# A 5x5 grouped convolution on sixteen tiles of TensorE: one product of each round cut in two

## The chip, the cores and the metric

The kernel runs on one core of a Trainium2 chip. The metric is the time of one execution on the device, in microseconds (us); the time given is the median of several executions. A profile is one more execution, recorded instruction by instruction. PE is TensorE (its matmuls; PEld are its weight loads), DVE is VectorE, ACT is ScalarE, POOL is GpSimd, and SP is the engine that issues most of the transfers.

## What is computed

Two layers work on an image of 4 batches, 512 channels and 64 x 64 pixels. The change lies in the first, a linear attention with two sets of heads: one set comes from a 1x1 projection of the image, the other from that projection after a 5x5 depthwise convolution and a small grouped 1x1 convolution:

```python
q, k, v = h @ wq.T, h @ wk.T, h @ wv.T
qkv = concatenate([q, k, v])
dw = conv(qkv, dw_kernel, groups=3 * 512)        # 5x5, one kernel per channel
pw = conv(dw, pw_kernel, groups=3 * 64)          # 1x1, within a head of 8 channels
f = concatenate([qkv, pw]).reshape(B, heads, 24, N)
query, key, value = relu(f[:, :, :8]), relu(f[:, :, 8:16]), f[:, :, 16:]
scores = einsum('bhdn,bhen->bhde', value_with_ones, key)
out = einsum('bhde,bhen->bhdn', scores, query)
out = out[:, :, :-1] / (out[:, :, -1:] + EPS)
y = x + batchnorm(proj_kernel applied to out)
```

The second layer takes edge filters of y, mixes them with 1x1 products, and normalises over the channels.

## The kernel before

The channels of the first layer are worked on in 16 groups (4 batches by 4 groups of 16 heads). For each group the kernel projects keys and values (`project`, L262, and `values`, L285), then queries, eight strips of 512 pixels each. `project` also writes each strip into an image `inp` with borders (L283), for keys and for queries; the convolution reads that image. For values no convolution is made: a correlation with the convolved keys takes its place (`correlate`, L447, with `weigh`, L469).

`convolve` (L394) computes one half of the image of 32 channel sets at once. It runs four times in each group (keys and queries, two halves), so 64 times in all. It takes four banks of PSUM from a pool of four (`quad_tiles`, tag "quad"), the same four buffers that `correlate` and `spread_out` use. The depthwise 5x5 and the 1x1 kernel are folded into one set of weights (`mat`, built on POOL at L247). Ten rounds follow, for five horizontal shifts `dx` in the order 0, -2, -1, 1, 2 and two vertical blocks `b`. A round is sixteen products of 32 x 32 weights: head set i (0 to 3) reads partitions 32i to 32i+31, pixel set j writes partitions 32j to 32j+31 of bank i. So each of the sixteen products of a round works on its own 32 x 32 tile of the array, and the sixteen can run at the same time; the next round works on the same sixteen tiles. A product covers eight rows of 64 columns (512), or of 62 or 63 where the shift cuts off the edge (496, 504). All numbers are 32 bit, and the trace shows each product as two pairs of a weight load and a matmul, a first and a second pass; hence 20480 records for 10240 products. Below, tile n is the tile of the n-th product of a round, counted from 0.

After the ten rounds ScalarE reads the four banks (L415 for keys, in eight parts, with sums; L421 for queries, in four).

The order of PE's work is written out by hand: `keys_and_values` (L563) and `queries` (L593) list the steps, and after each step `advance` lets the stages that trail behind (projection of the heads L661, edge branches L738, fusing L848) issue a share of their own products, by fixed costs. The convolution's cost in these lists is a constant (T_CONV), so the order depends on no measured time. The last part of the kernel, from about 4.35 ms, has no convolution in it.

Of the kernel before, what the change touches and what calls it, by code (L numbers as in the profile page):

```python
# [50 lines left out]
KV_ORDER = (1, 0, 2, 3, 4, 5, 6, 7)  # L51
Q_ORDER = (6, 7, 5, 4, 3, 2, 1, 0)
DXS = (0, -2, -1, 1, 2)
VROW = 4 * 66


# [27 lines left out]
def _span(d, n):  # L84

    return max(0, -d), n - max(0, d)
# [3 lines left out]
def conv_seq_kernel(  # L90
    ctx: ExitStack, tc, x, wqkv, dpk, wtab, proj, projc, pwk, bn0, consts, vec, watt1, batt1, watt2, wbr, wfuse, out
):
    nc = tc.nc
# [15 lines left out]
    def work_tile(name, n=512):  # L109
        return work.tile([P, 512], F32, tag="w", name=name)[:, :n]  # L110
# [4 lines left out]
    def quad_tiles(name):  # L115
        return [psum.tile([P, 512], F32, tag="quad", name=name) for _ in range(4)]

    def squares(ap):

        return ap.rearrange("p (b x n) -> p n x b", b=4, n=4)  # L120

    def rows(ap, width=W):
        return ap.rearrange("p (r c) -> p r c", c=width)
# [21 lines left out]
    inps = {}  # L145
# [15 lines left out]
    def near_border(v):  # L161

        zeros = vals.tile([P, 8 * VROW], F32, name="zeros", tag="vals")
        nc.gpsimd.memset(zeros, 0.0)
        cols = v.rearrange("a b x r d -> (a b) x (r d)")
        for at in (0, W + 2):
            nc.sync.dma_start(out=cols[:, at : at + 2, :], in_=zeros[0 : 2 * NB, 0 : 2 * VROW])
        for b, r in ((0, 0), (NB - 1, 2)):
# [54 lines left out]
    first = ExitStack()  # L223
    x_first = first.enter_context(tc.tile_pool(name="x_first", bufs=12, side="right"))

    class Group:
# [167 lines left out]
        def convolve(self, t, half):  # L394
            banks = quad_tiles("cv")
            last = len(DXS) * 2 - 1
            for n, (dx, b) in enumerate((dx, b) for dx in DXS for b in range(2)):
                c0, c1 = _span(dx, W)
                for j in range(4):
                    for i in range(4):  # L400
                        q = slice(32 * i, 32 * i + 32)
                        nc.tensor.matmul(  # L402
                            rows(banks[i])[32 * j : 32 * j + 32, :, c0:c1],
                            lhsT=self.mat[t][q, j, (dx + 2) * 8 + 4 * b : (dx + 2) * 8 + 4 * b + 4, :],
                            rhs=inps[t][q, j, 8 * half + b : 8 * half + b + 8, c0 + dx : c1 + dx],
                            start=(n == 0), stop=(n == last),
                        )
            outs = []
            for i in range(4):
                o = work_tile("co")  # L410
                if t == KEY:
                    if half == 0 and i == 0:
                        self.ksum = mini.tile([P, 4, 4], F32, name="ksum")
                    for a in range(2):
                        nc.scalar.activation(  # L415
                            o.rearrange("p (n a x b) -> p a n x b", n=4, a=2, b=4)[:, a],
                            squares(banks[i][:, 256 * a : 256 * a + 256]), AF.Relu,
                            accum_out=self.ksum[:, 2 * half + a, i : i + 1],
                        )
                else:  # L420
                    nc.scalar.activation(o, banks[i], AF.Relu)  # L421
                outs.append(o)
            self.conv[t] = outs
# [10 lines left out]
        def load_near(self, count):  # L434

            for _ in range(count):
                half, jp, b = at = next(self.nears, (None,) * 3)
                if half is not None:
                    self.near[at] = vals.tile([P, 8 * VROW], F32, name="near", tag="vals")
                    for part in range(4):  # L440
                        v = self.near_dram[jp, 8 * half + b + 4 * (part // 2), 32 * (part % 2)]
                        nc.sync.dma_start(
                            out=self.near[at][32 * part : 32 * part + 32, :],
                            in_=bass.AP(v.tensor, v.offset, [[4 * VROW, 8], [(W + 4) * VROW, 4], [1, 8 * VROW]]),
                        )
# [514 lines left out]
    for n, cur in enumerate(groups):  # L960
# [5 lines left out]
        if n and n % NG == 0:  # L966
            last = groups[n - 1]
# [8 lines left out]
    last = groups[-1]  # L976
# [142 lines left out]
```

## Time and profile before

| | |
|---|---|
| median of three executions | 5017.47 us (5010.55 to 5027.52) |
| the profiled execution, its own time | 5033.35 us |
| its span, first to last instruction | 5031.6 us |
| mean clock that TensorE was granted | 0.971 |
| PE busy, matmuls | 4694.3 us (93%), 46140 records |
| DVE, ACT, POOL busy | 2083.3, 1581.8, 397.3 us |
| products of the convolution (L402) | 20480 records, 728.3 us busy, 36.0 us idle before them |
| weight loads of the convolution (L402) | 20480 records, 419.8 us busy, 313.1 us idle before them |
| 16 DMA engines, mean rate | 172 GB/s |

The page sums up busy time by engine, then gives the costliest groups of instructions: a row names the line, engine and operation, what is written and read, the shape, and the number; then busy time, the mean duration of one, the idle time of the engine ahead of such instructions, and what ended most of it. Matmuls overlap, so busy time is less than number times duration. "issue" as a cause of idle time means that nothing the profile shows was waited for. Other views used below are the answer for one source line, the timeline of a stretch (start, length, engine, line, operation, number, and in brackets the idle time before), and the trace's single records, with the start and length of each weight load, matmul and DMA packet.

### The profile page before, as it was taken

The numbers are of one execution on the slowest core, as the hardware profiler recorded it, in microseconds if no ns is written. First come the engines' busy times: TensorE is split into PE (matmuls) and PEld (weight loads), VectorE is DVE, ScalarE is ACT, GpSimd is POOL, SyncE is SP. The second block draws the span as 40 slices with busy tenths as digits, with TensorE's granted clock in tenths as the row PEclk, the third lists the DMA queues.
The fourth block names the chain that finished last, engine by engine and source line by source line (L and its number), as shares of the span: only waits on it lengthen the run. The fifth ranks groups of instructions, "written<-read, shape, count | busy, mean of one in ns | idle before, by whom it ended". The sixth has DMA issues, their size and how long they took to land. (4 is left out here: it accounts for less than half of the span.)

```text
span 5031.6 us, 106279 instructions
## 1 busy us (share of the span) xinstructions
PE 4694.3 (93%) x46140; PEld 2689.2 (53%) x46140; DVE 2083.3 (41%) x2761; ACT 1581.8 (31%) x2712; POOL 397.3 (8%) x298
## 2 busy tenths in 40 slices
PE   9999999999999999799899999989999899899887
PEld 5655654455666554354465656445446565444333
DVE  1222222115565533311355553441125555447955
ACT  2112111003454423200245442430014445214765
POOL 0000000000000012100000000220000000000445
PEclk9999999999999999899999999999999999899998
DMA  6434467775666566677565566647665555575435
GB/s 198 138 119 134 134 192 194 162 163 161 193 190 189 180 187 189 192 177 167 152 189 189 186 192 183 207 153 217 149 173 176 171 173 170 162 166 144 165 125 163
DMA packets 627940, 864.04 MB, mean 172 GB/s; under 512 B 324073, under 2 KB 381449, under 8 KB 609041
## 3 DMA queue, kind: packets, MB, share of 16 engines
q1 hardware_dynamic: 548880, 756.51, 52.4%
q10 hardware_dynamic: 78592, 100.74, 6.3%
q8 instruction: 362, 5.93, 0.5%
q14 instruction: 106, 0.86, 0.1%
HBM read 575.93 MB, written 213.98 MB: 157 GB/s over the span
## 5 line engine op out<-in xcount | busy, mean ns | idle before, releaser
L268 PE MATMUL proj<-xt,w_sb 128*128 128x512 f32 x2048 | 955.9, 610 | 56.7 <-DMA xt<-in_x 34.6
L661 PE MATMUL yps<-hd,fold_sb 128*128 128x512 f32 x2048 | 907.8, 599 | 18.5 <-DMA hd<-heads 16.2
L402 PE MATMUL cv<-inp,mat 32*32 32x512 f32 x20480 | 728.3, 593 | 36.0 <-issue 28.2
L268 PEld LDWEIGHTS proj<-xt,w_sb 128*128 128x128 f32 x2048 | 382.7, 194 | 528.0 <-issue 451.6
L661 PEld LDWEIGHTS yps<-hd,fold_sb 128*128 128x128 f32 x2048 | 386.1, 191 | 511.0 <-issue 458.8
L402 PEld LDWEIGHTS cv<-inp,mat 32*32 32x32 f32 x20480 | 419.8, 103 | 313.1 <-issue 151.9
L848 PE MATMUL zps<-ef,wf_sb 128*128 128x512 f32 (+1 forms) x1056 | 473.4, 601 | 36.4 <-DMA ef<-ef 19.4
L290 PEld LDWEIGHTS val<-w_sb,xt 128*128 128x128 f32 x4096 | 470.6, 192 | 33.2 <-issue 25.9
L290 PE MATMUL val<-w_sb,xt 128*128 128x128 f32 x4096 | 485.2, 277 | 0.1
L738 PE MATMUL br<-maps,wbr_sb 128*128 128x256 f32 (+1 forms) x1792 | 474.2, 418 | 3.7 <-DVE s_sb L335 2.9
L274 ACT COPY strip<-proj 128x512 f32<-128x512 f32 x256 | 149.3, 583 | 932.5 <-PE proj L268 912.0
L666 DVE SCALAR_TENSOR_TENSOR yt<-yps,shift,xr 128x512 f32<-128x512 f32 x128 | 96.0, 750 | 836.5 <-PE yps L661 780.0
L738 PEld LDWEIGHTS br<-maps,wbr_sb 128*128 128x128 f32 x1792 | 340.9, 193 | 146.9 <-issue 102.0
L457 PE MATMUL corr<-near,ckt 128*32 128x160 f32 x8192 | 333.7, 315 | 40.3 <-DMA near<-near 32.9
L848 PEld LDWEIGHTS zps<-ef,wf_sb 128*128 128x128 f32 x1056 | 205.3, 198 | 285.5 <-issue 235.9
L247 POOL TENSOR_TENSOR mat<-dp_sb 128x1280 f32<-128x1280 f32 x32 | 76.7, 2398 | 3484.8 <-PE cv L402 2882.9
L457 PEld LDWEIGHTS corr<-near,ckt 128*32 128x32 f32 x8192 | 257.2, 111 | 136.1 <-issue 78.6
L714 DVE TENSOR_TENSOR maps<-dv 128x1054 f32<-128x1054 f32 (+1 forms) x112 | 158.0, 1411 | 376.3 <-PE br L738 376.2
L318 ACT ACTIVATE kt<-tr 128x512 f32<-128x512 f32 x128 | 75.9, 593 | 529.8 <-PE tr L316 401.2
L366 DVE RECIPROCAL rec<-rec 128x512 f32<-128x512 f32 x64 | 214.4, 3351 | 1.7
L746 ACT ACTIVATE ef_o<-br,shift,scale 128x256 f32<-128x256 f32 (+1 forms) x224 | 131.4, 590 | 228.1 <-PE br L738 210.4
L415 ACT ACTIVATE co<-cv 128x256 f32<-128x256 f32 x256 | 94.0, 398 | 331.1 <-PE cv L402 310.6
(127 smaller groups left out, 4049.2 us busy)
## 6 DMA issues: line engine op xcount, KB each, us to landing
xt<-in_x SPq DMA_DIRECT2D x316, 512.0 KB
near<-near SPq DMA_DIRECT2D x512, 264.0 KB
inp<-strip ACTq DMA_DIRECT2D x1024, 64.0 KB
win<-y SPq DMA_DIRECT2D x96, 396.0 KB
near<-vt SPq DMA_DIRECT2D x512, 66.0 KB
y<-yt SPq DMA_DIRECT2D x128, 264.0 KB
heads<-q SPq DMA_DIRECT2D x128, 256.0 KB
cheads<-cq SPq DMA_DIRECT2D x128, 256.0 KB
```

What stands on the lines that cost most here:

```text
L268: nc.tensor.matmul(ps, lhsT=self.w[t][:, c, :], rhs=xs[self.b, j][c], start=(c == 0), stop=(c == NCH - 1))
L274: nc.scalar.copy(s, ps)
L290: nc.tensor.matmul(ps[:, ts(c, P)], lhsT=xs[self.b, j][n][:, ts(c, P)], rhs=self.w[VALUE][:, n, :], start=(n == 0), stop=(n == NCH - 1),)
L366: nc.vector.reciprocal(rec, rec)
L402: nc.tensor.matmul(rows(banks[i])[32 * j : 32 * j + 32, :, c0:c1], lhsT=self.mat[t][q, j, (dx + 2) * 8 + 4 * b : (dx + 2) * 8 + 4 * b + 4, :],
L457: nc.tensor.matmul(self.banks[jj][32 * i : 32 * i + 32, 160 * b : 160 * b + 160], lhsT=self.held["c", i][:, at : at + 32], rhs=v[:, 4 * n ...
L661: nc.tensor.matmul(ps, lhsT=fold_sb[g // NG][:, g % NG, ts(c, P)], rhs=hd[g], start=(g == 0), stop=(g == 2 * NG - 1),)
L666: nc.vector.scalar_tensor_tensor(yt[:, :, 1 : W + 1], rows(ps), shift0[:, c : c + 1], rows(xr), ALU.add, ALU.add)
L714: nc.vector.tensor_sub(flat[:, half : 3 * half - 2], dvs[:, 2 : 2 * half], dvs[:, 0 : 2 * half - 2])
L738: nc.tensor.matmul(rows(ps), lhsT=wbr_sb[:, k, c, :], rhs=rows(maps[:, slot[k], c % 2, :], WB)[:, :, 0:W], start=(c == 0), stop=(c == NCH ...
L746: nc.scalar.activation(o[:, n, :], parts[n], AF.Gelu, bias=shift1[:, k : k + 1], scale=scale1[:, k : k + 1], accum_out=pool_sb[:, k, u : u ...
L848: nc.tensor.matmul(ps, lhsT=wf_sb[:, k, ts(c, P)], rhs=ef[k], start=(k == 0), stop=(k == 3))
```

## The change

The first product of each round (i = j = 0) covers all its columns but the last twelve of each of the eight rows. The fifteen others follow unchanged. Then a second product with the same weights covers the twelve columns left over. The start mark stays with the first part in the first round (the second part never carries one), and in the last round the end mark of that tile moves to the second part. Nothing else is edited: other engines' instructions keep their order, and ScalarE's first read of the convolution's banks now waits for the second part, which has become the last product.

```diff
+TAIL = 12
...
         def convolve(self, t, half):
             banks = quad_tiles("cv")
             last = len(DXS) * 2 - 1
+
+            def product(n, dx, b, j, i, c0, c1, first=True, end=True):
+                q = slice(32 * i, 32 * i + 32)
+                nc.tensor.matmul(
+                    rows(banks[i])[32 * j : 32 * j + 32, :, c0:c1],
+                    lhsT=self.mat[t][q, j, (dx + 2) * 8 + 4 * b : (dx + 2) * 8 + 4 * b + 4, :],
+                    rhs=inps[t][q, j, 8 * half + b : 8 * half + b + 8, c0 + dx : c1 + dx],
+                    start=(n == 0 and first), stop=(n == last and end),
+                )
+
             for n, (dx, b) in enumerate((dx, b) for dx in DXS for b in range(2)):
                 c0, c1 = _span(dx, W)
+
                 for j in range(4):
                     for i in range(4):
-                        q = slice(32 * i, 32 * i + 32)
-                        nc.tensor.matmul(
...
-                            start=(n == 0), stop=(n == last),
-                        )
+                        lead = i == j == 0
+                        product(n, dx, b, j, i, c0, c1 - TAIL if lead else c1, end=not lead)
+                product(n, dx, b, 0, 0, c1 - TAIL, c1, first=False)
```

## The prediction

> **What bounds the kernel now.** I read the page first. PE is busy for 93% of the span, DVE for 41%. The convolution's products (L402) are the third costliest group: 728.3 us busy and 36.0 us idle before them. Queue q8, which brings instructions, matters later: 362 packets of 5.93 MB are 16 KB each, 256 instructions of 64 bytes.
>
> ```profile
> span 5031.6 us, 106279 instructions
> ...
> PE 4694.3 (93%) x46140; PEld 2689.2 (53%) x46140; DVE 2083.3 (41%) x2761; ACT 1581.8 (31%) x2712; POOL 397.3 (8%) x298
> ...
> q8 instruction: 362, 5.93, 0.5%
> ...
> L402 PE MATMUL cv<-inp,mat 32*32 32x512 f32 x20480 | 728.3, 593 | 36.0 <-issue 28.2
> ```
>
> Next the answer for L402 alone: its weight loads (PEld) sat idle mostly for "issue", waits that no semaphore explains.
>
> ```profile
>   issue: 180.0, 370
>   DVE weighed L475: 19.9, 30
> ```
>
> Then the timeline of weight loads in one undisturbed convolution: 32 loads in 0.23 us, stops of 0.2 to 0.3 us, and ten rounds done 10.6 us after the start.
>
> ```profile
> 191.67 0.23 PEld L402 LDWEIGHTS cv<-inp,mat 32*32 32x32 f32 x32 [0.17 <-issue]
> 192.13 0.10 PEld L402 LDWEIGHTS cv<-inp,mat 32*32 32x32 f32 x1 [0.22 <-issue]
> 192.56 0.55 PEld L402 LDWEIGHTS cv<-inp,mat 32*32 32x32 f32 x32 [0.32 <-issue]
> 193.42 8.02 PEld L402 LDWEIGHTS cv<-inp,mat 32*32 32x32 f32 x255 [0.31 <-issue]
> ```
>
> Last a disturbed one, which begins at 305.20 and takes 14.9 us: twice PE stops for over 2 us.
>
> ```profile
> 313.71 0.24 PEld L402 LDWEIGHTS cv<-inp,mat 32*32 32x32 f32 x32 [2.17 <-issue]
> ...
> 319.63 0.14 PEld L402 LDWEIGHTS cv<-inp,mat 32*32 32x32 f32 x4 [2.42 <-issue]
> ```
>
> The trace's single records of the 191.68 convolution give the rest. Each product is two pairs of weight load and matmul. A pass streams 0.83 ns a column plus 3 (430 ns for 512 columns, 423 for 504, 416 for 496), and 22 more for the first pass of a product whose tile was already free. When nothing waits, the next product starts 16.6 ns later. But where a product finds its tile of the array busy, the next product starts only 193 ns after that one does: in round 1 the first tile starts at 883 (453 + 430), and the second, free at 890, at 1076. One to three such stops fall in each round, so the last pass starts 10,070 ns after the first (1007 a round), where a tile's own two passes need 832 to 860. Some twenty convolutions show 10,070 to within 2 ns.
>
> [...] second passes of round 0 start at 453 to 553, after first passes of later products. [...] in the 305.20 convolution a packet starts at 311.39, PE stops 0.05 later and resumes at 313.71, 1.45 after the packet landed.
>
> **The change, part by part.** *Removed:* 12 of some 63 columns (8 rows, 96 of 504) from tile 0's leading product. Its two passes become 416, 400 or 408 columns for shifts of 0, 2 and 1: 350, 337, 343 ns. *Added:* one product of 96 columns a round, behind the fifteen; 640 products, 2560 PE instructions on 92,280 (2.8%; 6.25% within a convolution). No DMA, no SP or POOL step moves. ScalarE's first read of a convolution now waits for the tail, the last product, and its later reads have no waits on PE: the four last products it waited for started within 50 ns of each other, so nothing (at most 64 x 50 ns, 3 us, if a read waits for the tail alone).
>
> *A round after.* Tile 0: first pass 22 + 350, second 350; then the tail, queued long before, starts at 722. It is the one product that finds its tile busy. The next round's first product comes 193 later, at 915. The tail itself needs 2 x 83 = 167, up to 211 if each pass pays the 22 (bounds; 33-column passes of L327 follow each other on one tile every 33 ns, 27.5 + 5, so I take 167). So the stop lies over the tail. The second tile is free at 17 + 450 + 430 = 897 and wanted at 932: 35 ns to spare, so no further stop. Rounds: 915, 888, 901 for 512, 496, 504 columns. Start of the last round: 2 x 915 + 2 x 888 + 4 x 901 + 888 = 8098; its sixteenth product starts 249 later and ends after 438 + 416: 9201. Before: 10,070 + 416 = 10,486. **Gain 1.285 us** a convolution. If the tail took 211, the next product would wait too, one more stop per round but at 933 and not at 1007: about 1.0.
>
> *How many get it.* In 17 of the 64, tile 3 starts 0.7 to 4.9 us after tile 0, because its bank waits for VectorE (mostly L475). There the late tile sets the end and tile 0 is ahead: nothing gained. 47 x 1.285 = **60 us**.
>
> *What takes it back: instructions.* A 256-instruction block lasts four rounds, 4.03 us; with 68 a round and 894 ns it lasts 3.37. For the 138 blocks that are used up within a convolution (the block before mostly in it too) I took from the records the time from the previous block's change to 1.4 us after the landing (stopped PEs resumed 1.3 to 1.65 after it). Quartiles: 3.3, 4.0, 5.2 us. 67 of 138 are over 4.03, by 0.62 us in the mean over all; 102 are over 3.37, by 1.02. I hold these fetch times independent of PE's pace. The 47 clean convolutions: 117 blocks x 0.62 = 73 us late before, of which 42 show (they take 515 us against 47 x 10.07 = 473): 0.57 of it, the rest lay under the stops. After: 125 blocks x 1.01 = 126 us, of which 0.57 (72) to all (126) shows. With fewer stops to lie under I take 0.7: 88, a loss of 88 - 42 = **46 us**. The 17 staggered ones run 6.25% more instructions through the same fetch: 17 x 0.16 blocks x 0.7 = **2 us**.
>
> *Sum.* 60 - 46 - 2 = 12 to 13 us off. Against its own execution: 5033.35 us (span 5031.6 and 1.75 around it) becomes 5020.5. That execution stands 0.3% above the median of 5017.47; the same taken from the median gives **5004 us**. PE is the bound on both sides of the convolutions. Waits on PE for x (34.6 us) and near (32.9) could swallow a few us; I take none.
>
> **Rivals.** *Fetch doesn't hold it back* (blocks come sooner when asked sooner, or runs without the profiler fetch faster): up to the whole 60 us, 4957; with a quarter lost, 4972, which I take. For it: some twenty convolutions have no stop for instructions at all. Against: half of the blocks are late already. *Slower: fetch is the bound.* If all lateness shows, 126 - 42 = 84 is lost against 60 gained: 24 and 2 make 5043. It decides once more than 0.8 of the lateness shows, or blocks are over 0.2 us later than above. For it: the 6.25% more instructions come in full, and 102 of 138 blocks would be late. Against: a stop frees all tiles, and part of it stays covered. *The change doesn't do what it says*: another product takes over the 193 ns stop, at the 35 ns margin, every round; then the rounds stay near 1007, and only the fetch of more instructions remains: 5017 to 5022.
>
> **Chances.** Fetch-limited gain 0.50 (4989 to 5014, own range); nearly the full gain 0.27; slower by fetch 0.15; stop taken over 0.08. A measurement of this kernel can tell about 0.3% (15 us) from no change. Faster by more: 0.27 and 0.21 of the first, 0.48. Within: 0.28 of the first and the 0.08, 0.36. Slower: 0.15 and 0.01 of the first, 0.16. The range, 4960 to 5030, leaves out the far ends of the second and third.
>
> **What would show it.** In undisturbed convolutions the last pass starts at about 8870 instead of 10,070; 17 staggered ones keep their length; the "issue" idle of L402's loads loses its 0.2 to 0.3 us pieces and gains in pieces over 1 us; q8 has 10 more packets. I am wrong if rounds don't fall to about 900, if the stops over 1 us neither grow nor multiply, or if they swallow more than 60 us.

## The result, and the profile after

The kernel became slower: 5057.62 us median of four runs (5042.51 to 5065.52), beside 5018.39 us (5010.55 to 5027.52, four runs) for the kernel before. The ratio is 1.0077, with a 95% interval of 1.0058 to 1.0095. The prediction, 5004 us and more likely faster than not, was wrong in sign, and 5057.62 lies above its range.

The page of the changed kernel (the product is at L402 again, by chance; lines ahead of `convolve` stand two higher, later ones nine):

```profile
span 5040.7 us, 108783 instructions
...
PE 4708.8 (93%) x47420; PEld 2667.3 (53%) x47420; DVE 2086.8 (41%) x2761; ACT 1581.3 (31%) x2712; POOL 400.7 (8%) x298
...
q8 instruction: 372, 6.09, 0.5%
...
L402 PE MATMUL cv<-inp,mat 32*32 32x512 f32 (+2 forms) x21760 | 758.2, 573 | 46.1 <-issue 38.3
```

The 1280 added weight loads and 1280 added matmuls and the ten added packets on q8 are there: 256 PE instructions for each added packet of 16,384 bytes, by estimate 64 bytes an instruction. VectorE, ScalarE and GpSimd are busy as long as before. The products of L402 take 30 us more busy time (728.3 to 758.2) and 10 us more idle time (36.0 to 46.1): the loss lies in the convolutions. The two profiled spans differ by 9.1 us only, because the execution profiled before was slower than any timed run of its kernel and the one profiled after the fastest of its own; the medians say 39 us.

The answer for L402 alone says what the loads waited for (us, times):

```profile
  issue: 326.3, 790
  DVE weighed L484: 19.2, 31
```

"issue" goes from 370 pieces of 180.0 us to 790 of 326.3. VectorE is as before. Part of that growth is the view's: this answer leaves out gaps of up to 0.15 us. The page's row for the loads has every gap, and there the idle time rose by 57 us, from 313.1 to 370.1:

```profile
L402 PEld LDWEIGHTS cv<-inp,mat 32*32 32x32 f32 x21760 | 404.9, 103 | 370.1 <-issue 288.0
```

The timeline of weight loads of an undisturbed convolution, one without a stop for instructions or for a late bank, shows where the pieces lie:

```profile
371.24 0.48 PEld L402 LDWEIGHTS cv<-inp,mat 32*32 32x32 f32 x33 [0.17 <-issue]
371.96 0.72 PEld L402 LDWEIGHTS cv<-inp,mat 32*32 32x32 f32 x34 [0.24 <-issue]
372.93 1.31 PEld L402 LDWEIGHTS cv<-inp,mat 32*32 32x32 f32 x37 [0.24 <-issue]
374.44 0.73 PEld L402 LDWEIGHTS cv<-inp,mat 32*32 32x32 f32 x34 [0.20 <-issue]
375.49 0.74 PEld L402 LDWEIGHTS cv<-inp,mat 32*32 32x32 f32 x34 [0.31 <-issue]
376.55 0.74 PEld L402 LDWEIGHTS cv<-inp,mat 32*32 32x32 f32 x34 [0.32 <-issue]
```

Before, this view showed up to three stops at the opening and then 255 loads in one piece. Now every round ends in a stop: 34 loads (17 products) in 0.74 us, 0.32 us of nothing, and again. The period is 1.06 us, where I had predicted 0.89 to 0.92.

The stop itself is neither new nor longer. Before, the loads' waiting was spread over gaps too short for the view. The single records show it: a product that finds its tile idle has a first pass 22 ns longer, and such products begin together behind each stop. In the undisturbed convolutions at 191.68 (before) and 371.24 (after), in ns from the start:

```
                                     before                  after
groups of such products begin at     4243 5303 6364 7424     4253 5313 6374 7436
matmuls from one to the next           34   34   34            34   34   34
groups in the whole convolution        10                      10
matmuls from the last group on         16                      32
```

In both kernels 34 matmuls, 17 products, pass in a period of 1061 ns (at 504 columns). Sixteen products take 16/17 of that, an estimate of 998 ns a round; the prediction's 1007 is the time to the last start divided by ten. Seventeen products take the whole period. Both convolutions need ten periods, and before the last is only half filled, so the last start moves by little.

I call the length of a convolution the time from the start of its first matmul to the start of its last. Twenty of 64 take 10,070 ns before (sum of all 64: 724.8 us); after, nine take 10,217 to 10,230 (sum: 764.8 us). The sum grew by 40.0 us, as much as the medians lost. The single records of the convolution at 371.24, in ns from its start, beside what the prediction's steps say:

```
                              measured   predicted
tile 0, first pass                   0           0
tile 0, second pass                373         372
tail, first pass                   723         722
tail, second pass                  908         805
next round's first product         990         915
next round's second product       1083         932
```

Up to the start of the tail the prediction is within 1 ns. The tail's second pass then starts not 83 ns after its first, when the columns are through, but 185 ns after it.

### The profile page after: what moved, and what is told of

It reads as the page before. It is cut to its first block, busy times and chain, and to the rows that moved or that the text cites. A ratio compares the mean times of both kernels' runs of the same rounds, so it can differ in the third digit from the quotient of the medians.

```text
span 5040.7 us, 108783 instructions
## 1 busy us (share of the span) xinstructions
PE 4708.8 (93%) x47420; PEld 2667.3 (53%) x47420; DVE 2086.8 (41%) x2761; ACT 1581.3 (31%) x2712; POOL 400.7 (8%) x298
## 5 line engine op out<-in xcount | busy, mean ns | idle before, releaser
L402 PE MATMUL cv<-inp,mat 32*32 32x512 f32 (+2 forms) x21760 | 758.2, 573 | 46.1 <-issue 38.3
L402 PEld LDWEIGHTS cv<-inp,mat 32*32 32x32 f32 x21760 | 404.9, 103 | 370.1 <-issue 288.0
```

The lines of the kernel that those rows point to most:

```text
L402: nc.tensor.matmul(rows(banks[i])[32 * j : 32 * j + 32, :, c0:c1], lhsT=self.mat[t][q, j, (dx + 2) * 8 + 4 * b : (dx + 2) * 8 + 4 * b + 4, :],
```

## Theories

**Q, the count.** The expectations call it a queue; no record shows one. Q is an estimate, made from two lengths and to be tested by others. Sixteen products of two loads and two matmuls are 64 instructions of PE, entries below; seventeen are 68. Suppose that entries have their turn in program order, and none before the one 64 places ahead is done with: a load 101 ns after its start (its measured length), a matmul 185 ns after its last column. The 185 ns are read from the record above. The entry 64 ahead of the tail's second pass is tile 0's second pass of the same round, behind which the tail starts at 723 on that tile; the tail's second pass starts at 908, and 908 - 723 = 185. The prediction's "193 ns stop" of the kernel before fits the same estimate. There the tile's next product starts at 883, when its previous one has ended, so the turn of its second pass comes at 883 + 185 = 1068; the next product stands behind it in the order and starts at 1076. That a count of entries is what holds them back is the supposition; the records show the starts.

I wrote this as a small recurrence by hand: 64 entries, the 101 and 185 ns, and from the records 0.83 ns a column plus 3 for a pass, and 22 more on an idle tile. It gives 10,086 ns before and 10,223 after; with 185 ns, counts of 60, 62, 66 or 68 don't give both. These two lengths were used to find it; the lengths of the experiments were predicted from it.

**W**, the prediction's own reading: the 193 ns come after any product that finds its tile busy, so the columns of the cut decide. **F**: only the fetch of 6.25% more instructions costs time (372 packets instead of 362).

## Experiments

The chip of these runs has the kernel before at 4992.28 us (25 runs; 4993.23 in the second group), 0.5% under the first chip. The expectations were written on the first chip's level unless they give ratios, so their microseconds are compared as shares of 5018.39.

**Width of the cut (tail24).**

```diff
-TAIL = 12
+TAIL = 24
```

> The change with 24 columns in the tail instead of 12; the number of instructions is that of the change. Theory Q (queue): [...] A round of before has 16 x 4 = 64 entries, a round of the change has 68[...]: an undisturbed convolution stays at 10.22 us from first to last first-pass start, as with 12 columns, and the time stays within 0.3% of the changed kernel's (5043 to 5073 us). Theory W (the prediction's): a product that finds its tile busy holds the next one back by 193 ns, and how wide the cut is decides who finds its tile busy; 24 columns leave tile 0 free 10 to 20 ns a column earlier and the last pass starts at 8.75 us instead of 9.5 (same model, tail's second pass late): over 30 us less than the changed kernel. Theory F (instruction fetch alone): no difference from the changed kernel, since as many instructions are fetched.

Measured: 5028.26 us, ratio 1.0072 (1.0047 to 1.0097), as the change's 1.0077. Undisturbed convolutions take 10,212 ns. Twice the width changes nothing, which Q and F allow and W doesn't.

**One product fewer, without and with the cut (drop1, tail_drop1).** The second has the same condition in the changed kernel.

```diff
                 for j in range(4):
                     for i in range(4):
+                        if n and 4 * j + i >= 15:
+                            continue
...
-                            start=(n == 0), stop=(n == last),
+                            start=(n == 0), stop=(n == last or 4 * j + i >= 15),
```

> The kernel before with one product (tile 15) left out in rounds 1 to 9 of every convolution, so part of the sum is not computed. Q: 60 entries a round[...]: 9.57 us from first to last start in an undisturbed convolution instead of 10.07 (10.09 by the same model), 0.5 us x 64 = 33 us less, and up to some 20 us more for 2304 instructions that need not be fetched: 4965 to 4990 us. W: the stops are between the tiles 0 to 14, which are there as before: 10.05 us, nothing gained in clean convolutions. F: 10.07 us too, only the share of fetch stops shrinks by 6%, 4 us or so.

> The changed kernel with one product (tile 15) left out in rounds 1 to 9 of every convolution, so part of the sum is not computed: the cut of tile 0 with its tail is there as in the change, but a round has 16 products and 64 entries again. Q: 10.07 us from first to last start in an undisturbed convolution, as in the kernel before, and its time, 5005 to 5030 us. W: the tail still takes the stop, or loses it, as in the change: 9.5 us by the same model, or the 10.22 that the change has. F: as before.

Measured: drop1 4970.17 us, ratio 0.9952 (0.9931 to 0.9973), 9557 ns. tail_drop1 4987.00 us, ratio 0.999 (0.998 to 1.0001), 10,060 ns. Both lengths and tail_drop1's time came as Q has them. The time of drop1 fell by less than expected, which as a ratio was 0.989 to 0.994: its convolutions are together 31 us shorter than in the profile of before, the time 22. The granted clock may be some 7 of the difference, an estimate (0.972 in the mean of its runs, 0.974 in the kernel before's on this chip). Their timelines of one undisturbed convolution each, drop1 first:

```profile
192.40 0.23 PEld L404 LDWEIGHTS cv<-inp,mat 32*32 32x32 f32 x32 [0.17 <-issue]
192.85 0.10 PEld L404 LDWEIGHTS cv<-inp,mat 32*32 32x32 f32 x1 [0.23 <-issue]
193.28 8.36 PEld L404 LDWEIGHTS cv<-inp,mat 32*32 32x32 f32 x269 [0.32 <-issue]
```

```profile
194.21 0.48 PEld L402 LDWEIGHTS cv<-inp,mat 32*32 32x32 f32 x33 [0.17 <-issue]
194.94 0.72 PEld L402 LDWEIGHTS cv<-inp,mat 32*32 32x32 f32 x32 [0.24 <-issue]
195.90 8.08 PEld L402 LDWEIGHTS cv<-inp,mat 32*32 32x32 f32 x257 [0.24 <-issue]
```

This is the decisive pair. In drop1 the tiles 0 to 14 have the same work in the same order as before, and lose half a microsecond; by W nothing happens to them. In tail_drop1 the cut and its tail are all there, but a round has 64 entries again; in the single records the stop comes every 34 matmuls and 1060 ns, and no longer at the end of each round. Length and time are those of the kernel before. The two also settle a rival, that the columns to be streamed set the length: both stream the same columns, and tail_drop1, with the four entries of the cut more a round, takes 503 ns longer. The cut itself costs nothing and brings nothing: the seventeenth product costs. One more or one fewer isn't symmetric: four entries fewer save 513 ns, four more cost 148. The periods say why: the records of drop1 have nine groups, those of before and of the change ten.

**Four products fewer (drop4).** As drop1, with `>= 12`.

> The kernel before with four products (tiles 12 to 15) left out in rounds 1 to 9 of every convolution, so a quarter of the sum is not computed. Q: 48 entries a round, [...] a convolution falls to the tiles' own pace: 8.69 us from first to last start instead of 10.07, some 85 us over 64 convolutions, and less fetch (9216 instructions, 36 blocks), so 4890 to 4935 us. W: tiles 0 to 11 stop one another as before: 10.0 us, at most the fetch is saved: 4985 to 5015.

Measured: 4920.84 us, ratio 0.9855 (0.9834 to 0.9877), 8678 ns.

```profile
191.82 0.23 PEld L404 LDWEIGHTS cv<-inp,mat 32*32 32x32 f32 x32 [0.17 <-issue]
192.27 0.10 PEld L404 LDWEIGHTS cv<-inp,mat 32*32 32x32 f32 x1 [0.22 <-issue]
192.70 7.48 PEld L404 LDWEIGHTS cv<-inp,mat 32*32 32x32 f32 x215 [0.32 <-issue]
```

At 504 columns a round now takes 845 ns (one tile's leading passes start at 4249 and 5094 in this convolution), the tiles' own two passes of 423: the number of entries no longer bounds it. Twelve tiles stop one another no longer, against W. The 64 convolutions together are 128 us shorter than in the profile of before, but the time fell by 71, to a ratio just above the expected 0.974 to 0.983. Some of it is the clock: TensorE was granted 0.970 in the mean of these runs and 0.974 in the kernel before's on the same chip, and 0.004 x 4921 is 20 us, an estimate. About the rest stands in PE's idle time elsewhere (span less PE busy and less the idle time ahead of the convolution's products): 312 us here, 270 in tail_drop1.

**The tail in the middle (mid9).**

```diff
                         product(n, dx, b, j, i, c0, c1 - TAIL if lead else c1, end=not lead)
-                product(n, dx, b, 0, 0, c1 - TAIL, c1, first=False)
+                        if 4 * j + i == 9:
+                            product(n, dx, b, 0, 0, c1 - TAIL, c1, first=False)
```

> The change with its twelve columns behind the tenth product of the round instead of behind the sixteenth: the same work and the same 68 entries a round in another order. Q (64 entries in order): [...] the model gives 10.52 us from first to last start of an undisturbed convolution against 10.22 for the change and 10.09 for before: some 19 us more than the change over 64 convolutions, 1.010 to 1.014 of before. W (193 ns behind a product that waits): 10.29 to 10.3 against 9.5 for the change by the same model, which the change itself did not show. F (fetch alone): as the change, 1.0077.

Measured: 5025.76 us, ratio 1.0058 (1.0038 to 1.0078), 10,501 ns in 18 convolutions. The length is Q's within 0.2%, against W, which wants 10,300; but the time is a miss. An undisturbed convolution is 0.28 us longer than in the change, which should have cost 18 us, and the kernel is no slower than the change (1.0077, interval 1.0058 to 1.0095). The missing microseconds are in the disturbed ones, taken up next.

**A constant in place of a load (near_before, near_after).**

```diff
-                    for part in range(4):
-                        v = self.near_dram[jp, 8 * half + b + 4 * (part // 2), 32 * (part % 2)]
-                        nc.sync.dma_start(
...
-                        )
+                    nc.gpsimd.memset(self.near[at], 0.25)
```

> The kernel before, in which the tile near is filled with a constant by GpSimd instead of loaded by 512 transfers of 264 KB, so the correlation uses other data. With those transfers gone from the DMA engines, instruction packets should land sooner: the 35 stops of 63 us for instructions inside the convolutions fall to under half if the transfers delay them, and the 33 us that PE waits for near go too: 4910 to 4970 us. If the packets' time has nothing to do with that traffic, the stops stay at about 60 us and the time at 4950 to 4985. Clean convolutions stay at 10.07 us in every theory.

> The same edit on the changed kernel, so the correlation uses other data here too; the number that tells is its time less that of near_before. F (all the loss is instruction fetch): with the stops gone the difference goes too, 0 to 5 us. Q with the fetch stops on top: 64 x 0.15 = 10 us stay in clean convolutions at 10.22 us, and each remaining stop costs about 0.26 us more than before[...] (worked out by putting single stops into the model): 10 to 25 us, against 39 with the transfers there. If the transfers don't delay the packets: 35 to 40 again.

Measured: near_before 4898.88 us, ratio 0.9813 (0.9788 to 0.9837); near_after 4912.60 us, 0.9836 (0.9815 to 0.9857). The difference is 13.7 us, against 39 with the transfers there. Undisturbed convolutions take 10,077 and 10,219 ns. The same rows of the two pages, near_before first:

```profile
q1 hardware_dynamic: 528400, 618.08, 44.5%
...
q8 instruction: 362, 5.93, 0.5%
...
L402 PE MATMUL cv<-inp,mat 32*32 32x512 f32 x20480 | 726.5, 595 | 26.2 <-issue 15.5
```

```profile
q1 hardware_dynamic: 528400, 618.08, 44.8%
...
L402 PE MATMUL cv<-inp,mat 32*32 32x512 f32 (+2 forms) x21760 | 745.5, 569 | 28.4 <-issue 17.2
```

The same instructions are fetched, beside 618 MB on q1 instead of 757, and the idle time for "issue" ahead of these matmuls falls from 28.2 to 15.5 us in the kernel before and from 38.3 to 17.2 in the changed one. Without the transfers there are fewer stops: 27 of 38.9 us instead of 42 of 67.5 in the kernel before. What links the two isn't shown. A packet takes 1007 ns from start to landing in the median before and 1021 in near_before, so it isn't faster under way, and when it was asked for the trace doesn't show. The stops did not fall to under half, as expected. The ratio of near_before lies in its range (0.978 to 0.990), but the working under that range had only stops and waits for near in it. The time fell by 94 us: some 33 of waits for near, 12.5 off the convolutions (724.8 to 712.3), and the clock, which I hadn't counted. On this chip TensorE was granted 0.974 in the runs of the kernel before and 0.980 here, and 0.006 x 4899 is about 30 us. The waits for x fell as well, from 34.6 to 6.9. Together these estimates are over 94; the profile of before is from the first chip, so the sum can't be closed.

**Half the instructions (rows64).** In `convolve`:

```diff
+                if b:
+                    continue
...
-                        q = slice(32 * i, 32 * i + 32)
+                        q = slice(64 * (i // 2), 64 * (i // 2) + 64)
...
-                            start=(n == 0), stop=(n == last),
+                            start=(n == 0), stop=(n == last - 1),
```

> The kernel before with 64 rows of the array a tile instead of 32 and five rounds instead of ten: two tiles of the 4 x 4 grid act as one, half of the convolution's instructions are gone, and it sums other data than the convolution's. Each column of tiles streams as many columns as before. It asks what a layout would be worth that filled 64 rows. Q: 64 entries now are two products for each of 8 tiles[...]: 9.0 us from first to last start instead of 10.07, about 70 us less, and half the convolutions' instructions need no fetch, up to some 30 us more: 4890 to 4930 us. W: at a busy tile each second product is followed by a wait of 193 ns or more: no faster than before. F: only the 30 to 45 us of fetch are saved.

Measured: 4897.09 us, ratio 0.9805 (0.9784 to 0.9827), 9002 ns in 46 of 64 convolutions.

```profile
q8 instruction: 282, 4.62, 0.4%
...
L404 PE MATMUL cv<-inp,mat 64*32 64x512 f32 (+2 forms) x10240 | 636.5, 589 | 5.0 <-DVE cq L560 2.5
```

No stop of over 0.45 us that follows an instruction packet is left in the convolutions. It is no version of the kernel, but it says what the entries cost: the same streaming a tile in half the entries takes 1.07 us less a convolution.

**All lengths together.** The excess is the sum of the 64 lengths less 64 undisturbed ones. A stop counts if over 0.45 us lie between the starts of two loads and an instruction packet landed 1.15 to 1.8 us before the second (resumption is mostly 1.3 to 1.65 us after the landing); its length is that distance.

```
             entries  length, ns       at that   excess   stops for
             a round  Q       measured length    us       instructions
before       64       10,086  10,070   20 of 64   80.4    42, 67.5 us
after        68       10,223  10,218    9        110.8    56, 87.9
tail24       68       10,223  10,212   11        102.0    45, 73.3
mid9         68       10,522  10,501   18         80.5    40, 63.0
tail_drop1   64       10,073  10,060   19         82.0    43, 69.4
drop1        60        9,572   9,557   21         82.2    40, 65.2
drop4        48        8,692   8,678   32         41.5    15, 20.4
rows64       32*       9,008   9,002   46         26.3     0
near_before  64       10,086  10,077   25         67.4    27, 38.9
near_after   68       10,223  10,219    9         77.9    28, 42.7
* one product for each of its eight tiles
```

One recurrence with two fitted constants, count and delay, gives all ten lengths within 0.2%. Two of them were used to find it, tail24 and the near runs repeat these two, and five are new. The new ones are needed: if the delay may be fitted as well, counts of 60 (135 ns) and 66 (195 ns) also give the first two within 0.2%. In a recurrence from the terms above with products 16.6 ns apart, of all counts from 56 to 75 only 63 and 64 come within 0.5% of every length. So the count is an estimate of 63 or 64 from the lengths; what keeps it isn't shown.

The excess is the larger part of the loss. It is not all instructions: the 17 to 19 convolutions whose banks come late hold 38 us of it before and all of it with rows64. Nor is it free of the clock. TensorE was granted 0.5 of its clock for 12 us within the convolutions before, 24 after, 22 in tail24 and 20 in mid9, which by estimate costs at most half of that; taking it off leaves 74 before, 99 after, 91 in tail24 and 71 in mid9. With the tail last the excess still rises, by 17 to 24 us (22 to 30 as it stands), and with the same number of instructions but the tail in the middle it doesn't. Each figure is from one trace. So the count of instructions alone, theory F, doesn't explain it. I put single stops of the instruction flow into the same recurrence, at all places of a convolution in turn, and took the mean loss. A stop of 0.2 us costs 0.08 us before, 0.17 after and 0.01 with the tail in the middle; one of 0.4 us costs 0.19, 0.35 and 0.12; one of 2 us costs 1.67, 1.93 and 1.72. In the model, entries have their turn with time to spare before and in mid9, and a stop is partly hidden; with the tail last, less of it is. The records agree: of the twenty convolutions that took 10,070 ns before, five took 10,285 to 10,383 after, as they would if stops of some tenths of a microsecond or less now showed. This part is a model that fits afterwards, not an experiment of its own: mid9 was run before I had it.

## Why the prediction was wrong

**The step that failed** is "The tail itself needs 2 x 83 = 167, up to 211 if each pass pays the 22", with the reading under it, "where a product finds its tile of the array busy, the next product starts only 193 ns after that one does". The times were read rightly; the rule drawn from them was a rule about tiles, and what the runs support is a count of entries: with the tiles' work left alone, drop1 loses 513 ns. The tail took 990 - 723 = 267 ns, outside both bounds; by Q because its second pass was entries 67 and 68 of the round. My bounds came from passes of L327 that follow each other every 33 ns; the duration was right (the second pass took 82 ns of the 267), and the wait wasn't in that row.

**"So the stop lies over the tail"** fails with it. By Q the wait doesn't lie over anything: with 68 entries a round, the entry 64 ahead of a product lies one product less than a round back, and the product's turn waits for that one. Later rounds repeat it exactly, at 504 columns: the tail starts at 4586, its second pass 183 later, the next lead 114 after that, that lead's second pass 422 later and the next tail 342 after that, 1061 ns in all. The 35 ns to spare for the second tile never came into play: it started at 1083 instead of 932.

**"Gain 1.285 us a convolution", 60 us** became a loss of 0.148 us: 64 x 0.148 = 9.5 us.

**"In 17 of the 64 ... nothing gained"**, and that these keep their length, also failed. Two of them that have few stops for instructions went from 10,870 to 11,024 and from 10,791 to 11,027.

**Instruction fetch, 46 + 2 us lost.** The direction was right and the premise wrong. A block of 256 instructions lasted as long as before, by estimate 3.99 us at 504 columns (four rounds of 998 ns, or 3.76 of 1061), not 3.37. The excess grew by 110.8 - 80.4 = 30.4 us in the profiled pair (21.6 for tail24). Up to 6 of that is by estimate the clock; that the rest is stops less hidden is the model's reading. Of the 30 us, 20 stand in more and longer stops (67.5 to 87.9 us). That is a little too much, since the ordinary stop of the changed kernel, 0.42 us between starts, is just under the 0.45 from which a stop counts; stops of over 1 us, which the prediction had asked about, grew from 29 of 58.0 us to 37 of 75.6. How much of that was chance in the transfers' timing stays open, since tail24 fetches the same instructions with 73.3 (31 of 63.6 over 1 us). The stops for instructions weren't hidden throughout: 42 of 67.5 us before, none with half the convolution's instructions (rows64).

Together 9.5 + 30.4 is the 40 us by which the convolutions of the profiled pair grew, and the medians lost 39. Outside the convolutions that pair differs by 31 us the other way. About 15 of these are by estimate the clock (282 us at a granted 0.5 there before, 252 after, half of which is lost), and 15 are PE's idle time that isn't ahead of the convolution's products (301 to 286 us).

**What held:** 10 more packets on q8, no other engine's work changed, and ScalarE was busy as long as before. What its first read of the banks lost by waiting for the tail wasn't measured apart. "The issue idle loses its 0.2 to 0.3 us pieces" turned out the other way: they multiplied, because the waiting of a period now falls in pieces that are long enough for the view to show.

**The rivals.** The one closest in place was "the change doesn't do what it says: another product takes over the stop", with 0.08; it kept rounds at 1007 and the time at 5017 to 5022. It was right that a stop stays in every round; it missed that a round with one product more takes the whole period of 1061. The one closest in time was "fetch is the bound", 5043; it would have had rounds near 900 and more than 0.8 of the lateness showing, and rounds of 1061 refute it. No rival counted entries.

## What to carry to other kernels

Ask of a gap that comes once per round not only who is busy, but how many instructions lie between two events that keep the same distance: an estimated 64 here, loads counted. Splitting an instruction to even out work adds entries, and here entries were the scarce thing: four more a round cost 148 ns of an undisturbed convolution, one product of sixteen fewer saved 513, and the same streaming a tile in half the entries (rows64) 1068. Look at single records too: a view that leaves out short gaps made a stop look new that had only been spread. Test a reading of a stop with a change that leaves the supposed cause alone and alters the count, before building on it.

## What the runs showed of the hardware that was not expected

- A stream of small products on 16 tiles was bounded by the number of its loads and matmuls: at 504 columns 34 matmuls and their loads, 68 entries, took 1061 ns in both kernels, so that a round took about 998 ns with 64 entries and 1061 with 68. With 48 entries it took 845, the tiles' own pace. A count of 64 entries, with 185 ns behind a matmul's last column, gives all ten lengths within 0.2%; both are estimates from these lengths and the starts at 723 and 908 ns, and what keeps the count isn't shown.
- With the tail last, the disturbed convolutions lost more than with it in the middle, at the same number of instructions: an excess of 102 to 111 us against 80.5 (91 to 99 against 71 without the half clock). That stops are less hidden with the tail last is what the model says of it: 0.17 us lost to a stop of 0.2 us, 0.08 before and 0.01 with the tail in the middle.
- Without the 512 transfers of 264 KB, stops for instructions in the convolutions fell from 67.5 to 38.9 us in the kernel before, and from 87.9 to 42.7 in the changed one, though a packet took no less time from start to landing (1007 and 1021 ns in the median, before and near_before).
